# One weight chunk's scaling on VectorE, split spread rows, a 128-row mask product and a new order in an adaptive-norm block

## The chip, the cores and the metric

The kernel runs on one core of one Trainium2 chip. The metric is the device time of one execution in microseconds (us); the median of several runs is compared. The core has five engines that matter here: TensorE (PE in the profile, its weight loads PEld), VectorE (DVE), ScalarE (ACT), GpSimd (POOL), and SyncE (SP), which only issues transfers. Each works through its own list of instructions in order and waits on semaphores for the others.

## The reference

The kernel computes one transformer block with modulation from a condition vector, in float32 (cut to what matters here):

```python
mod = (_silu(L0_c) @ L0_wmod).reshape(L0_c.shape[0], 6, 1, -1)
sa, ca, ga, sb, cb, gb = (mod[:, 0], mod[:, 1], mod[:, 2], mod[:, 3], mod[:, 4], mod[:, 5])
ga = (2 * (ga >= 0) - 1) * jnp.maximum(jnp.abs(ga), 0.25)     # gb likewise
h = _layernorm(x, axis=-1) * (1 + ca) + sa
x = x + ga * _L0_attn_ref(h, ...)
h = _layernorm(x, axis=-1) * (1 + cb) + sb
x = x + gb * _L0_ffn_ref(h, L0_ffn_weight, L0_ffn_bias)
```

`x` has 8 batches of 1024 rows of 512. `_L0_ffn_ref` quantizes rows and weight in blocks of 32 to a small grid (6-bit values times a scale for each block) and multiplies. In `_L0_attn_ref` the reshape from heads back to rows puts what is not zero into the first 16 rows of each batch: the attention's result there comes from three rounds on 16 of 32 columns of each head, and all the other rows get only the bias `bo`.

## The kernel before, in words

So there are two branches. The long one takes the 1008 other rows of each batch: 16 groups, two for each batch, of 4 tiles of 128 or 124 rows. A group `g` goes through four steps. `load` brings x and adds the gate row `g2B` (gate times `bo`); in mode "P" the addition is an instruction for each tile, in mode "A" ScalarE copies the gate row into the tile and the transfer accumulates x onto it. `NV[g]` says how many of a group's four additions are on VectorE (with the row sum as a by-product, so that ScalarE needs no pass for the mean); the others are on GpSimd. `front` makes the norm (two ScalarE passes for each tile, small GpSimd steps for the inverse root, two VectorE steps with the rows psA and psB), the largest value of each block, and the two quantizing products on GpSimd (`q<-x,I`, `x<-q,M`); then TensorE transposes the tile into a psT bank, ScalarE rounds it to `xh`, VectorE makes the rest `xl`. `back` multiplies with the weight: for each of 4 output chunks 12 matmuls (xh with wh and wl, xl with wh) into a psO bank, which ScalarE evicts to `y`; an accumulating transfer adds x, and a store ends the group.

The short branch, `attention`, takes the 128 first rows (16 of each batch) as one tile `xs`: norm with rows spread over the partitions, projections, three rounds of attention whose logits begin with a mask product `par` x `far` and whose 16 x 4 blocks are matmuls of 32 x 32, the output product, and then the same norm, quantizing and product as the others. It uses the two psX banks.

Ahead of both stands the preparation. The weight comes in 4 chunks: largest values, scales (`prep_scale`), then in `prep_w` a scaling product, a rounding step on VectorE, a product back, transposes and the split into `wh` and `wl`. The two products of chunk `o` are on VectorE if `o` is in `WVEC`, else on GpSimd. The modulation is products of the condition with sections of `wmod` (`mod_sums`). Their rows are spread over partitions by a product with a row of the selection matrix `sel`. The rows RA and RS of the long branch and of the short branch's second norm come from `split`: two parts in float32r, by a ScalarE and a VectorE step. The rows RSA and RA1 of the short branch's first norm come from `whole`: one ScalarE step, in float32. `row_s` makes the product that spreads a row for the short branch.

All transfers of the preparation are on SP's queue, in the order of a string (`ORDER`); the mask `pm` alone is on GpSimd's, since it changes the type.

The order is a planner's. `Program.record` collects all instructions with a cost for each; `issue` gives each a due time, worked back from the due times in `DUE` (by strand: "B3.1" is chunk 1 of group 3's product, "L4" the load of group 4, "it0" a round of attention) with the weights `LAM`, and then lists them engine by engine: of the instructions that would be ready, the most urgent one, or a short wait (`WP`, `WV`, `WS`, `WE`, `WG`) for one that is more urgent. So a change of these numbers changes the order on every engine.

All recorded instructions bear one line in the profile, L205 (the call in `record`), so groups are told apart by their tiles.

Of the kernel before, what the change touches and what calls it, by code (L numbers as in the profile page):

```python
# [16 lines left out]
P = 128  # L17
D = 512
# [4 lines left out]
SA, CA, GA, SB, CB, GB = range(6)  # L23
# [1 line left out]

RATE = 405.0

LAM = {"gpsimd": 0.52, "scalar": 2.743, "sync": 1.216, "tensor": 0.595, "vector": 4.946}
MU = 529.0
LAMD = 2.333  # L30

DUE = {
    "first": -1000000.0,
    "sa": -156334.0,
    "L2": -176869.0,
    "B0.0": 26895.0,
    "B0.1": 27074.0,
    "B0.2": 26975.0,
    "B0.3": 26841.0,
    "L4": -130933.0,  # L40
    "B1.0": 38540.0,
    "B1.1": 38578.0,
    "B1.2": 32192.0,
    "B1.3": 38380.0,
    "att0": 47675.0,
    "kv0": 58850.0,
    "it0": 69907.0,
    "kv1": 81199.0,
    "it1": 92374.0,
    "kv2": 103548.0,  # L50
    "it2": 114723.0,
    "end": 109565.0,
    "end2": 120740.0,
    "B2.0": 53637.0,
    "B2.1": 47871.0,
    "B2.2": 53571.0,
    "B2.3": 53341.0,
    "B3.0": 76200.0,
    "B3.1": 65668.0,
    "B3.2": 64751.0,  # L60
    "B3.3": 65924.0,
    "B4.0": 76782.0,
    "B4.1": 80161.0,
    "B4.2": 79564.0,
    "B4.3": 78738.0,
    "B5.0": 91733.0,
    "B5.1": 92977.0,
    "B5.2": 93758.0,
    "B5.3": 91437.0,
    "B6.0": 104432.0,  # L70
    "B6.1": 127890.0,
    "B6.2": 146211.0,
    "B6.3": 105002.0,
    "F7": -6665.0,
    "B7.0": 117131.0,
    "B7.1": 117032.0,
    "B7.2": 116933.0,
    "B7.3": 116834.0,
    "L11": 45368.0,
    "B8.0": 136487.0,  # L80
    "B8.1": 136389.0,
    "B8.2": 135242.0,
    "B8.3": 136428.0,
    "B9.0": 139315.0,
    "B9.1": 139389.0,
    "B9.2": 142912.0,
    "B9.3": 139046.0,
    "B10.0": 155442.0,
    "B10.1": 157387.0,
    "B10.2": 157247.0,  # L90
    "B10.3": 155146.0,
    "L14": 106456.0,
    "F11": 79170.0,
    "B11.0": 167926.0,
    "B11.1": 167827.0,
    "B11.2": 167728.0,
    "B11.3": 167629.0,
    "L15": 89281.0,
    "F12": 101104.0,
    "B12.0": 180624.0,  # L100
    "B12.1": 195729.0,
    "B12.2": 196404.0,
    "B12.3": 178619.0,
    "B13.0": 193670.0,
    "B13.1": 194406.0,
    "B13.2": 192518.0,
    "B13.3": 184062.0,
    "B14.0": 195341.0,
    "B14.1": 205923.0,
    "B14.2": 204891.0,  # L110
    "B14.3": 205725.0,
    "B15.0": 218839.0,
    "B15.1": 216872.0,
    "B15.2": 218523.0,
    "B15.3": 218424.0,
}
START = {"tensor": 1070.0, "vector": 630.0, "gpsimd": 570.0, "scalar": 600.0, "sync": 600.0}

# [306 lines left out]
@with_exitstack  # L425
def _adaln(ctx: ExitStack, tc: tile.TileContext, t):
    ORDER = "0123AkCxSyXGsp"
    NV = [3, 2] + [0] * 14
    WARM3 = 0
    P0 = ((0,), (1,), (2, 3))  # L430
    P1 = ((0, 1), (2, 3))
# [2 lines left out]
    WARM2 = 0  # L434
    PARTS = 1
    REARLY = ()
    WVEC = ()
    WP = 1834
    WV = 0
    WS = 284  # L440
    WE = 235
    WG = 9256
    nc = tc.nc
    prog = Program(nc, tc)
    prog.wait, prog.gap = {"gpsimd": WP, "vector": WV, "scalar": WS, "tensor": WE}, WG
    V, S, G, PE, SY = (prog.engine(e) for e in ("vector", "scalar", "gpsimd", "tensor", "sync"))
# [3 lines left out]
    def new(name, shape, dt=F32):  # L450
        return sb.tile(shape, dt, name=name)
# [16 lines left out]
    psX = Ring("psX", 2, [P, D], F32, pp)  # L468
# [24 lines left out]
    first1, firstA, one16p = pka[:, 139:140], pka[:, 140:141], pka[:, 141:142]  # L493
# [50 lines left out]
    cs = new("cs", [P, 4, 32])  # L544
    G.memset(cs, 0.0)
    G.memset(eps, EPS)
    pm = new("pm", [2, P + D], F32R)
    G.dma_start(pm, t["pm"])
    G.memset(ones, 1.0)

# [101 lines left out]
    def split(name, ps, plus=False):  # L652
        r = new(name, [P, D], F32R)
        S.activation(r, ps, AF.Identity, scale=-0.5 if plus else 1.0, bias=one16 if plus else 0.0)
        V.scalar_tensor_tensor(r, ps, restA if plus else rest, r, ALU.mult, ALU.subtract)
        return r


    def whole(name, ps, plus=False):
        r = new(name, [P, D])  # L660
        if plus:
            S.activation(r, ps, AF.Identity, scale=firstA, bias=one16p)
        else:
            S.mul(r, ps, first1)
        return r


    vlr = Ring("vl", 2, [P, D])

    def flip(ps):  # L670
# [251 lines left out]
    def attention():  # L922
# [29 lines left out]
        ps = psX()  # L952
# [6 lines left out]
        for i in range(2):  # L959
            ps = psX()  # L960
# [25 lines left out]
        nm, r = ln_stats(xs)  # L986
# [3 lines left out]
        nm, r = ln_stats(h1)  # L990
# [5 lines left out]
        ps = psX()  # L996
# [82 lines left out]
        for it in range(3):  # L1079
# [213 lines left out]
```

## Time and profile before

| | |
|---|---|
| three runs | 301.08, 303.74, 301.57 us; median 301.57 |
| the profiled execution | 300.82 us, of which the span from first to last instruction is 299.0 |
| TensorE busy | 278.8 us (93% of the span), 2239 matmuls |
| weight loads | 216.1 us (72%) |
| VectorE busy | 225.3 us (75%) |
| ScalarE busy | 237.1 us (79%) |
| GpSimd busy | 239.7 us (80%) |
| granted TensorE clock | 0.963 in the mean |
| moved | 46.12 MB read, 16.78 MB written, 210 GB/s over the span |

The times of engines overlap, so none of them is a share of the span that could be saved by itself. A busy TensorE need not be at its peak, since ends of matmuls are modelled; where the rate matters, the step from one matmul's start to the next one's is the better number. Idle time of an engine costs only where something that ends the span waits for it.

### The profile page before, as it was taken

The page shows a single profiled execution, that of the slowest core. Times are in us where ns is not written, and L with a number is a line of the kernel's source. Part 1 is how long each engine was busy: PE and PEld are TensorE (multiplying, and loading weights), DVE is VectorE, ACT ScalarE, POOL GpSimd, SP SyncE. Part 2 cuts the span into 40 slices and gives each one's busy share as a digit, 9 for nine tenths or more (in the row PEclk, how much of TensorE's full clock was granted, in tenths as well). Part 3 has the DMA queues.
Part 4 walks back from the last instruction along what each step waited for, and adds up shares of the span by engine and source line. Part 5 has one row for each costly group of instructions (what it writes and reads, how often), then busy time and mean ns, then how long its engine had stood idle before and what let it go on. Part 6 is the DMA issues. An engine that isn't in the chain of part 4 may idle for free.

```text
span 299.0 us, 6185 instructions
## 1 busy us (share of the span) xinstructions
PE 278.8 (93%) x2239; PEld 216.1 (72%) x2239; DVE 225.3 (75%) x391; ACT 237.1 (79%) x541; POOL 239.7 (80%) x379
## 2 busy tenths in 40 slices
PE   7685599899999999999999999989999999999993
PEld 2333287799979777776787878766887788788782
DVE  6869686974989778977898799938796689941312
ACT  4169979998999999999899999979798699453400
POOL 2679989799599996999799999975999968897010
PEclk9786599999999999999999999999999999999998
DMA  6999995099569895738999657979599847576486
GB/s 223 341 410 390 273 305 167 0 181 260 185 158 212 294 212 187 136 139 158 275 246 255 136 191 138 260 216 208 196 176 311 203 179 136 170 212 139 170 153 263
DMA packets 14845, 63.28 MB, mean 212 GB/s; under 512 B 1630, under 2 KB 2398, under 8 KB 10848
## 3 DMA queue, kind: packets, MB, share of 16 engines
q0 software_dynamic: 3632, 25.99, 45.4%
q1 hardware_dynamic: 11184, 36.91, 32.0%
q8 instruction: 17, 0.28, 0.4%
q14 instruction: 12, 0.10, 0.1%
HBM read 46.12 MB, written 16.78 MB: 210 GB/s over the span
## 4 chain that ended last, share of the span: by engine, by line
PE 75%; POOL 8%; ACT 3%; issue 2%; DVE 1%; POOLq 0%; DVEq 0%
PE psO L205 52%; PE psX L205 13%; PE psT L205 9%; POOL x L205 4%; POOL q L205 2%; ACT L205 1%; ACT t L205 1%; POOL y L205 1%; ACT x L205 1%; ACT jk L205 0%; PE psB L205 0%; PE psA L205 0%; POOL s_u_l L205 0%; ACT y L205 0%; POOL cq L205 0%
## 5 line engine op out<-in xcount | busy, mean ns | idle before, releaser
L205 PE MATMUL psO<-xl,wh 128*128 128x512 f32 (+3 forms) x292 | 99.8, 389 | 0.0
L205 PE MATMUL psO<-xh,wh 128*128 128x512 f32 (+3 forms) x292 | 97.7, 386 | 1.5 <-ACT y L205 1.3
L205 PE MATMUL psO<-xh,wl 128*128 128x512 f32 (+3 forms) x292 | 97.8, 395 | 0.0
L205 POOL TENSOR_TENSOR x<-q,ms 128x512 f32<-128x512 fp8e4 (+1 forms) x64 | 73.6, 1258 | 0.1
L205 POOL TENSOR_TENSOR q<-x,s_I 128x512 fp8e4<-128x512 f32 (+1 forms) x64 | 72.4, 1204 | 1.0 <-DVE s_I L205 0.7
L205 ACT ACTIVATE y<-psO,cbT,gbT 128x512 f32<-128x512 f32 (+3 forms) x68 | 48.9, 722 | 23.1 <-PE psO L205 20.6
L205 PEld LDWEIGHTS psO<-xh,wh 128*128 128x128 f32 x292 | 52.7, 191 | 16.1 <-ACT y L205 3.5
L205 PE MATMUL psT<-pka,x 128*128 128x128 f32 (+1 forms) x256 | 56.0, 277 | 4.5 <-POOL x L205 4.5
L205 PEld LDWEIGHTS psO<-xh,wl 128*128 128x128 f32 x292 | 53.1, 189 | 9.4 <-issue 1.7
L205 PEld LDWEIGHTS psO<-xl,wh 128*128 128x128 f32 x292 | 52.8, 189 | 9.3 <-issue 1.2
L205 DVE TENSOR_TENSOR xl<-psT,xh 128x512 fp32r<-128x512 f32 (+1 forms) x64 | 41.1, 671 | 18.6 <-ACT xh L205 18.3
L205 DVE SCALAR_TENSOR_TENSOR x<-x,s_r_m,psB 128x512 f32<-128x512 f32 (+1 forms) x64 | 43.7, 741 | 11.2 <-POOL s_r_m L205 11.1
L205 DVE SCALAR_TENSOR_TENSOR x<-x,s_nm,psA 128x512 f32<-128x512 f32 (+1 forms) x64 | 45.2, 731 | 6.2 <-PE psA L205 3.9
L205 ACT ACTIVATE jk<-x,s_nm 128x512 bf16<-128x512 f32 (+1 forms) x64 | 46.3, 723 | 0.7
L205 PEld LDWEIGHTS psT<-pka,x 128*128 128x128 f32 (+1 forms) x256 | 35.1, 143 | 14.4 <-POOL x L205 6.9
L205 ACT ACTIVATE jk<-x 124x512 bf16<-124x512 f32 (+1 forms) x59 | 37.2, 630 | 3.5 <-POOL x L205 2.8
L205 ACT CAST xh<-psT 128x512 fp32r<-128x512 f32 (+1 forms) x64 | 34.6, 578 | 2.8 <-PE psT L205 2.3
L205 DVE TENSOR_REDUCE mr<-x 128x64 f32<-128x2048 f32 (+4 forms) x19 | 36.7, 1933 | 0.2
L205 POOL TENSOR_TENSOR x<-x,g2B 124x512 f32<-124x512 f32 (+1 forms) x19 | 25.2, 1361 | 0.2
L205 ACT COPY x<-g2B 128x512 f32<-128x512 f32 x40 | 22.6, 620 | 0.0
L205 POOL DMA_DIRECT2D y<-in_xT x15 | 13.6, 908 | 10.6 <-ACT y L205 10.5
L205 PE MATMUL psX<-ai,w 128*128 128x128 f32 x96 | 17.0, 274 | 0.0
(236 smaller groups left out, 369.2 us busy)
## 6 DMA issues: line engine op xcount, KB each, us to landing
x<-in_x POOLq DMA_DIRECT2D x10, 1024.0 KB, 10.6
y<-in_xT POOLq DMA_DIRECT2D x8, 1024.0 KB, 8.0
outT<-y SPq DMA_DIRECT2D x8, 1024.0 KB, 6.1
y<-in_xT POOLq DMA_DIRECT2D x7, 992.0 KB, 7.7
outT<-y SPq DMA_DIRECT2D x7, 992.0 KB, 7.2
x<-in_x SPq DMA_DIRECT2D x5, 1024.0 KB, 7.3
y<-in_wmod SPq DMA_DIRECT2D x16, 256.0 KB, 5.8
x<-in_wmod SPq DMA_DIRECT2D x8, 256.0 KB, 7.1
```

The lines of the kernel that those rows point to most:

```text
L205: o.fn = lambda: getattr(eng, meth)(*args, **kw)
```

## The change

It sets the two products of weight chunk 0 on VectorE, and all four gate additions of group 1 (two were there already). RSA and RA1 are made by `split` like the other rows, so that `row_s` always multiplies in float32r, and `whole` goes. The mask operands get 128 rows in place of 2, the added ones zero, and so does their transfer. The planner gets new due times, weights and waits. The diff, cut to its core (all of `DUE` has new values, some keys come and some go):

```diff
-LAM = {"gpsimd": 0.52, "scalar": 2.743, "sync": 1.216, "tensor": 0.595, "vector": 4.946}
+LAM = {"gpsimd": 0.528, "scalar": 2.496, "sync": 1.276, "tensor": 0.595, "vector": 4.937}
-LAMD = 2.333
+LAMD = 2.307
 DUE = {
...
-    "B0.0": 26895.0,
-    "B0.1": 27074.0,
+    "B0.0": 14381.0,
+    "B0.1": 13580.0,
...
-    "att0": 47675.0,
-    "kv0": 58850.0,
-    "it0": 69907.0,
+    "att0": 44379.0,
+    "kv0": 52784.0,
+    "it0": 65018.0,
...
-    NV = [3, 2] + [0] * 14
+    NV = [3, 4] + [0] * 14
...
-    WVEC = ()
-    WP = 1834
-    WV = 0
-    WS = 284
-    WE = 235
-    WG = 9256
+    WVEC = (0,)
+    WP = 1902
+    WV = 420
+    WS = 808
+    WE = 178
+    WG = 8719
...
-    pm = new("pm", [2, P + D], F32R)
+    pm = new("pm", [P, P + D], F32R)
...
-    def whole(name, ps, plus=False):
-        r = new(name, [P, D])
-        if plus:
-            S.activation(r, ps, AF.Identity, scale=firstA, bias=one16p)
-        else:
-            S.mul(r, ps, first1)
-        return r
...
-    RSA = whole("RSA", mod_sums(SA, psX()))
-    RA1 = whole("RA1", mod_sums(CA, psX()), True)
+    RSA = split("RSA", mod_sums(SA, psX()))
+    RA1 = split("RA1", mod_sums(CA, psX()), True)
...
-            PE.matmul(ps, lhsT=l.bitcast(F32) if r.dtype == F32 else l, rhs=r, start=True, stop=True)
+            PE.matmul(ps, lhsT=l, rhs=r, start=True, stop=True)
...
-    odd = np.stack([1 - odd, odd])
-    arr["pm"] = np.concatenate([odd[:, :P], -(2.0**100) * odd[::-1]], axis=1).astype(np.float32)
+    odd = np.stack([1 - odd, odd] + [0 * odd] * (P - 2))
+    arr["pm"] = np.concatenate([odd[:, :P], -(2.0**100) * odd[[1, 0] + list(range(2, P))]], axis=1).astype(np.float32)
```

More of the change, by code (lines that the diff above doesn't have):

```diff
@@ L26 @@
 RATE = 405.0
-LAM = {"gpsimd": 0.52, "scalar": 2.743, "sync": 1.216, "tensor": 0.595, "vector": 4.946}
+LAM = {"gpsimd": 0.528, "scalar": 2.496, "sync": 1.276, "tensor": 0.595, "vector": 4.937}
 MU = 529.0
-LAMD = 2.333
+LAMD = 2.307
 DUE = {
     "first": -1000000.0,
+    "w0": -177835.0,
+    "gb": -163184.0,
     "sa": -156334.0,
     "L2": -176869.0,
-    "B0.0": 26895.0,
-    "B0.1": 27074.0,
[L38 to L44, printed above, removed]
-    "att0": 47675.0,
-    "kv0": 58850.0,
-    "it0": 69907.0,
[L48 to L73, printed above, removed]
+    "B0.0": 14381.0,
+    "B0.1": 13580.0,
+    "B0.2": 16143.0,
+    "B0.3": 25635.0,
+    "L4": -137832.0,
+    "Q1": -111416.0,
+    "B1.0": 44936.0,
+    "B1.1": 44933.0,
+    "B1.2": 49148.0,
+    "B1.3": 53827.0,
+    "att0": 44379.0,
+    "kv0": 52784.0,
+    "it0": 65018.0,
+    "kv1": 76101.0,
+    "it1": 86920.0,
+    "kv2": 98124.0,
+    "it2": 110279.0,
+    "end": 104488.0,
+    "end2": 115707.0,
+    "L5": -101336.0,
+    "B2.0": 52569.0,
+    "B2.1": 47189.0,
+    "B2.2": 53125.0,
+    "B2.3": 57787.0,
+    "B3.0": 75107.0,
+    "B3.1": 70636.0,
+    "B3.2": 64915.0,
+    "B3.3": 65916.0,
+    "B4.0": 80773.0,
+    "B4.1": 81416.0,
+    "B4.2": 82211.0,
+    "B4.3": 79757.0,
+    "B5.0": 92096.0,
+    "B5.1": 88296.0,
+    "B5.2": 93710.0,
+    "B5.3": 92034.0,
+    "B6.0": 103659.0,
+    "B6.1": 127353.0,
+    "B6.2": 145615.0,
+    "B6.3": 104229.0,
@@ L74 @@
     "F7": -6665.0,
[L75 to L78, printed above, removed]
+    "B7.1": 124442.0,
+    "B7.2": 118816.0,
+    "B7.3": 115308.0,
     "L11": 45368.0,
[L80 to L92, printed above, removed]
@@ L93 @@
-    "F11": 79170.0,
[L94 to L114, printed above, removed]
@@ L115 @@
-    "B15.3": 218424.0,
+    "Q8": 32264.0,
+    "B8.1": 137319.0,
+    "B8.2": 136497.0,
+    "B8.3": 143922.0,
+    "B9.0": 121957.0,
+    "B9.1": 121795.0,
+    "B9.2": 127836.0,
+    "B9.3": 124088.0,
+    "L13": 63213.0,
+    "B10.0": 147572.0,
+    "B10.1": 156270.0,
+    "B10.2": 158092.0,
+    "B10.3": 140043.0,
+    "L14": 99823.0,
+    "F11": 79170.0,
+    "B11.0": 169421.0,
+    "B11.1": 175173.0,
+    "B11.2": 168888.0,
+    "B11.3": 171043.0,
+    "L15": 92811.0,
+    "F12": 99916.0,
@@ L116 @@
+    "B12.0": 181196.0,
+    "B12.1": 196536.0,
+    "B12.2": 197211.0,
+    "B12.3": 177629.0,
+    "Q13": 139881.0,
+    "B13.0": 193693.0,
+    "B13.1": 195475.0,
+    "B13.2": 178741.0,
+    "B13.3": 184700.0,
+    "F14": 143268.0,
+    "Q14": 164729.0,
+    "B14.0": 198000.0,
+    "B14.1": 206337.0,
+    "B14.2": 206132.0,
+    "B14.3": 206966.0,
+    "B15.0": 219327.0,
+    "B15.1": 247927.0,
+    "B15.2": 219246.0,
+    "B15.3": 219137.0,
 }
```

## The prediction

> **What bounds the kernel now.** I read the page first, then the busy times by stage, the chain of waits, and the timeline where the change acts. The head of the page:
>
> ```profile
> span 299.0 us, 6185 instructions
> PE 278.8 (93%) x2239; PEld 216.1 (72%) x2239; DVE 225.3 (75%) x391; ACT 237.1 (79%) x541; POOL 239.7 (80%) x379
> PEclk9786599999999999999999999999999999999998
> ```
>
> TensorE is busy for 93% of the span, and its clock is granted in full from the sixth of 40 slices on. Where it is not busy shows in the same times by stage (columns: window, its length, then busy us and instructions of PE, PEld, DVE, ACT, POOL; granted clock, DMA share, GB/s):
>
> ```profile
> 0.00:33.00 33.00, 21.48 (x126) 9.56 (x126) 26.03 (x70) 19.69 (x51) 22.31 (x41) 0.76 0.96 340
> 33.00:65.00 32.00, 30.08 (x213) 24.69 (x214) 25.74 (x46) 29.50 (x78) 28.99 (x72) 0.92 0.66 171
> 65.00:205.00 140.00, 138.34 (x1453) 110.13 (x1452) 116.58 (x186) 131.98 (x296) 126.72 (x185) 1.00 0.80 203
> ...
> 265.00:292.50 27.50, 27.30 (x138) 22.13 (x136) 6.26 (x11) 7.50 (x12) 10.33 (x11) 1.00 0.65 171
> ```
>
> There are two regimes. Up to 33 us TensorE has little to do: the DMA engines are 96% busy, and the other engines prepare weights, gates and group 0. From 33 us TensorE is the bound: it idles 32.00 - 30.08 = 1.9 us up to 65, then 1.7 us in 140. At the end the other engines have long finished. So TensorE time saved after 33 us is span saved, and so is an earlier start at 33 us; work moved among the others counts only if it shifts that start or makes TensorE wait.
>
> The chain of waits at the start (start, us, what), and its one bubble later:
>
> ```profile
> 28.70 1.27 POOL x L205
> 29.97 2.01 POOL q L205 x2
> 31.98 1.02 POOL x L205
> 33.04 2.12 PE psT L205 x8
> ...
> 194.21 1.50 issue
> ```
>
> The first transposes of group 0 wait for GpSimd, and ahead of its two quantizing products stands a 1.27 us addition `x<-x,g2B` of group 1. The 1.50 us late in the run is a pause in which TensorE's stream waits for nothing that the profile names.
>
> **The change, part by part.** The sum is made against the profiled execution: 300.82 us, of which 299.0 are span and 1.8 lie around it.
>
> (a) Spread rows. The rows of the short branch's first norm were made by `whole` in float32; `split` makes them float32r. A float32 row product runs as two instructions:
>
> ```profile
> 45.90 1.02 PE L205 MATMUL psX<-RA,sel 128*128 128x512 f32 x2
> 46.76 0.27 PE L205 MATMUL psT<-pka,x 128*128 128x128 f32 x1
> ```
>
> From its start to the next it takes 46.76 - 45.90 = 0.86 us. A float32r product of this width goes by every 0.23 us (start to start, psA and psB rows). Two such products: 2 x 0.63 = 1.26 us less TensorE time, in the stage where TensorE is the bound. Both ends of this price are known, so I take -1.26.
>
> What it adds is a VectorE step per row (RA from psA: 0.75 us), 1.5 us in all. For the second row it is in TensorE's way. In the new order the product of wmod that fills bank psX0 is followed by only eight transposes (0.11 each) and two half products (0.12 each), 1.1 us, before psX0 is written again; that write now waits for ScalarE (0.78), then VectorE (0.75) and three handovers of about 0.1, 1.8 us. TensorE, in order, waits 0.7 us, and behind it stand group 0's last pieces. If the transposes wait for GpSimd anyway, it is 0; if the VectorE step also stands behind the reduction ahead of it (1.2), it is 1.9. I take +0.7.
>
> (b) The mask product, three times. Timeline of TensorE around one:
>
> ```profile
> 102.53 0.38 PE L205 MATMUL psO<-xh,wh 128*128 128x496 f32 x1
> 102.85 0.49 PE L205 MATMUL psX<-pm 2*128 2x512 f32 x1
> 103.27 0.50 PE L205 MATMUL psO<-xl,wh 128*128 128x496 f32 x1
> ```
>
> The neighbours go by every 0.22 us. Here the step before it takes 0.32 (0.10 over) and its own 0.42 (0.19 over a 128-row product's 0.23). With 128 rows both should vanish: 3 x 0.28 = -0.84. The ends are -0.84 and 0, for no row shows this product with 128 rows; I take -0.84, since every 128-row product in the trace goes by in 0.23. The Trainium skill speaks against this gain: "TensorE: Matmul & The Clock Gate", section "LDWEIGHTS (loading the stationary operand)", says that a weight load's time follows the columns, not the rows of the contraction. By that rule alone two rows cost what 128 cost, and the sum would be 0.84 higher.
>
> (c) The start, up to 33.04 us. Group 1's four additions are now all on VectorE, so the 1.27 us addition at 28.70 is gone: -1.27 if the quantizing scales are there in time. They are due at about 28.5, and VectorE has two of those additions (0.7 each) less ahead of them, put behind. Against it stands the mask's load: 128 rows of 2,560 bytes, 0.33 MB in place of 5 KB, issued at 1.31 on GpSimd's queue, ahead in time of nearly all loads. The DMA engines are full from 3 us to 33 and move about 390 GB/s (410 and 390 in the page's third and fourth slices), so what lands afterwards lands 0.84 us later, and TensorE and ScalarE wait for those loads (wmod's first section lands at 10.36, and TensorE waits 1.7 us for it in all). I take -1.27 + 0.84 = -0.43. The ends: -1.27 with the load hidden; +1.1 with the addition's place filled by something else, the load in full, and 0.26 us from the scaling. That scaling, two products of chunk 0 (about 0.7 each on VectorE, 1.05 on GpSimd), is otherwise costed at nothing: GpSimd was idle after it from 10.34 to 12.25, and VectorE, 26.03 busy of 33, gets 1.4 us more. If that cover is gone, chunk 1's scale is late by up to 1.4 us and GpSimd's next product with it.
>
> The product of the first wmod section that stood between transposes and group 0's products (35.09 to 36.96) moves some products later. Before, ScalarE's copy (to 35.79) hid some 0.9 us of its 1.9; in its new place it costs 1.0, as its twin at 40.39. So nothing either way; half a microsecond if the clock comes up later.
>
> For the moved operations the trace has a warning:
>
> ```profile
> 9.29 1.05 POOL L205 TENSOR_TENSOR w<-q,ws 128x512 f32<-128x512 fp8e4 x1 [0.81 <-DVE q L205]
> 9.34 1.06 DVE L205 SCALAR_TENSOR_TENSOR wr<-ws,wM 128x48 f32<-128x48 f32 x1
> 10.43 0.21 DVE L205 SCALAR_TENSOR_TENSOR wr<-ws,wr 128x48 f32<-128x48 f32 x1
> ```
>
> Two steps of one shape: 1.06 us beside a GpSimd product, 0.21 alone. So a VectorE step that reads two tiles can stand still beside GpSimd. The Trainium skill has the rule, "SBUF — State Buffer", section "Who interferes with whom": such a VectorE step and a GpSimd step that reads SBUF exclude each other for the whole instruction. By it each of the four moved steps could hold GpSimd up for its 0.7 us, and the sum would be up to 2.8 higher.
>
> (d) The order anew. TensorE's instructions are as many as before, the tail's order is nearly the same, and on SP's queue a load of x and the short output each move ahead of one store. On GpSimd's queue the accumulating load into x4 moves between chunk 2's and chunk 3's products; it waits for four ScalarE copies, and behind it stand chunk 3's product and group 0's quantizing. ScalarE loses two accumulating passes (0.63 + 0.19) for two steps of 0.19: 1.3 us. The idle times of TensorE that a new order can touch are 0.30, 0.99 and 0.22 at 56.8, 59.5 and 61.8, together 1.5: there evictions stood on ScalarE behind copies into x1, which now stand earlier, but the norm's last step now directly follows an eviction, with 1.1 us of TensorE work against 1.6 of ScalarE's: a new wait of about 0.5. And evictions that end the smaller waits may stay: I take -0.7, ends -1.5 and +1.0. The pause at 194.21 has no cause in what is changed: 0, ends -1.5 and +1.5.
>
> The sum: -1.26 + 0.7 - 0.84 - 0.43 - 0.7 = -2.53, so 298.3 for the profiled execution. The median of the three runs is 301.57, 0.75 above that execution; so the forecast is 301.57 - 2.53, about 299.0 us.
>
> **The rivals.** First, faster by over 1%: VectorE's second spreading is covered (0), the start gains its whole 1.27, and the three waits go: -1.26 - 0.84 - 1.27 - 1.5 = -4.9, 296.7 us. For it: GpSimd, which ended the chain at the start, loses four large steps, and ScalarE 1.3 us. Against it: VectorE gains six large steps (two scalings, two additions, two spreadings) before 50 us, where it is 26.03 busy of 33 and 25.74 of 32 us.
>
> Second, slower: the accumulating load on GpSimd's queue. Its four copies (0.62 each, 2.5) now stand together on ScalarE behind chunk 1's copy; uncovered, they hold chunk 3's product and group 0's quantizing. Price: 2.5 + 0.84 for the mask's load + 0.99 for its issue = 4.3 at the start, against -1.26 - 0.84 of TensorE: +2.2, 303.8 us. It decides from a start 2.1 us later, that is, first transposes after 35.1. For it: in this stage ScalarE is busy 10 of 10 us from 20 on. Against it: the copies need only the gate row, there at 22.95.
>
> Third, the 128-row mask product does no better than the two-row one: 0.84 less gain, 299.9 us. It ends on the forecast's side.
>
> **How the numbers follow.** A measurement of this kernel can tell about 1%, 3.0 us, from no change. Forecast with the third rival, a change within 1%: 0.46. The first rival: 0.39. The second, and a slower result in general: 0.15, nearly all of it over 1%. All good ends together give -6.9, all bad ones +4.7. Two in ten left outside, the range is 295.8 to 303.0: below it lies the first rival with the pause gone too, above it the second in full. For the forecast alone it is 298.0 to 300.5.
>
> **What would show it.** Right: row products of 0.23 where 0.86 stood; three mask products with 128 rows, each at 0.23; TensorE's last product about 2.5 us before 294.2; first transposes at 32 to 33 us. Wrong: transposes after 35 us; mask products still at 0.42; TensorE idle over 1 us ahead of the second use of psX0 in 45 to 50 us, or anew in the short branch's 32x32 products, which now stand some 4 us of TensorE work earlier.

## The result, and the profile after

The changed kernel took 303.94 us (median of 20 runs, 302.92 to 305.66), the kernel before 302.19 us in the same series (20 runs, 298.49 to 305.08). The ratio is 1.0082, 95% interval 1.0062 to 1.0101: slower by 0.8% (by the two medians 1.75 us, 0.6%). The ratio leaves out runs more than 1.5% above the fastest of their kernel, and since before's runs spread widely this takes out from 0 of 26 to 14 of 29 of them, depending on the series: ratios of different series are therefore not held against each other below, but the medians are. The forecast was 299.0 us with a range of 295.8 to 303.0, so the sign was wrong and the time lies outside the range. The profiled execution of the changed kernel took 302.92 us, 301.1 of them span.

The head of its page, and its row of instruction loads (queue: packets, MB, share of 16 DMA engines):

```profile
span 301.1 us, 6178 instructions
PE 277.1 (92%) x2237; PEld 216.6 (72%) x2237; DVE 231.0 (77%) x399; ACT 235.7 (78%) x539; POOL 235.1 (78%) x375
PEclk9688579999999999999999999999999999999999
...
q8 instruction: 17, 0.28, 0.4%
```

The work moved as the diff says: GpSimd has 4.6 us less, VectorE 5.7 us more, and TensorE is busy 1.7 us less. Yet the span is 2.1 us longer, so TensorE waits more. Busy times by stage say where (columns as in the prediction: window, its length, busy us and instructions of PE, PEld, DVE, ACT, POOL; granted clock, DMA share, GB/s). First three stages of before:

```profile
33.00:45.00 12.00, 11.96 (x79) 8.71 (x80) 8.98 (x18) 9.79 (x26) 11.08 (x32) 0.80 1.06 280
45.00:60.00 15.00, 13.35 (x97) 11.53 (x96) 12.76 (x24) 14.71 (x40) 12.91 (x36) 1.00 0.23 79
...
187.00:200.00 13.00, 11.50 (x177) 8.86 (x176) 8.36 (x15) 12.01 (x27) 11.44 (x18) 1.00 0.90 253
```

The same of the changed kernel, with the long stage between:

```profile
33.00:45.00 12.00, 10.56 (x62) 8.31 (x60) 10.99 (x25) 9.00 (x26) 10.53 (x28) 0.67 1.04 289
45.00:60.00 15.00, 13.09 (x98) 11.05 (x98) 12.51 (x26) 14.57 (x39) 10.96 (x34) 1.00 0.46 120
60.00:187.00 127.00, 126.82 (x1306) 103.50 (x1306) 107.46 (x174) 120.37 (x277) 118.09 (x175) 1.00 0.74 188
187.00:200.00 13.00, 10.22 (x166) 7.21 (x165) 11.97 (x19) 10.90 (x25) 5.08 (x11) 1.00 0.74 151
```

Two stages got worse. From 33 to 45 us TensorE does 62 matmuls where it did 79, at a clock of 0.67 where it was 0.80. From 187 to 200 us it idles 2.78 us where it idled 1.50. In the 127 us between it idles 0.18 us in all. A smaller loss follows: from 200 to 292 us it idles 0.84 us where it idled 0.04.

At the start the transposes come 1.9 us earlier than before (31.11, was 33.04), better than forecast, and then the lead goes (timeline of the changed kernel: start, us, engine, line, instruction; in brackets the idle time before it and what ended it):

```profile
29.66 2.95 DVE L212 SCALAR_TENSOR_TENSOR x<-x,g2B 124x512 f32<-124x512 f32 x1
29.73 2.32 POOL L212 TENSOR_TENSOR x<-q,ms 128x512 f32<-128x512 fp8e4 x2
31.11 2.11 PE L212 MATMUL psT<-pka,x 128*128 128x128 f32 x8 [1.88 <-POOL x L212]
...
34.67 1.44 PE L212 MATMUL psO<-xh,wh 128*128 128x256 f32 x5 [1.44 <-ACT xh L212]
```

A gate addition on VectorE takes 2.95 us: it ends 0.56 after both of GpSimd's products have ended. ScalarE's next norm step needs its sum, and the `xh` roundings that TensorE needs stand behind that step on ScalarE. So the first product starts at 34.67, and TensorE runs it at half clock until 40.9 us; before, the clock was up from 37.8. Lined up by the matmuls that are left, the two kernels are within some 0.4 us of each other at 66 us and within 0.2 at 187 (their orders differ, so this is no finer than that), and at the end the changed one is 2.1 us behind. So by 187 us nothing is left of the early start and of TensorE's smaller work, and the loss comes after that.

What is lost at the end is the pause of the prediction's first part, which has grown (TensorE's timeline of before; "issue" means that TensorE waited for nothing that the profile shows):

```profile
193.02 1.19 PE L205 MATMUL psX<-t,vl 32*32 32x32 f32 x116
195.71 0.31 PE L205 MATMUL psX<-t,vl 32*32 32x32 f32 x12 [1.50 <-issue]
```

The same of the changed kernel:

```profile
193.10 0.27 PE L212 MATMUL psT<-pka,x 124*128 124x124 f32 x1
195.72 0.40 PE L212 MATMUL psO<-xl,wh 128*128 128x512 f32 x1 [2.35 <-issue]
```

The pause is 2.35 us where it was 1.50, and it stands between other instructions. It is joined by smaller waits that before did not have: 0.43 at 189.82 (VectorE's transpose of the attention weights), 0.43 at 207.63 (ScalarE's eviction) and 0.29 at 237.36 (GpSimd's quantizing).

### The profile page after: what moved, and what is told of

The parts are those of the page before. It is cut to its first block, busy times and chain, and to the rows that moved or that the text cites. A ratio compares the mean times of both kernels' runs of the same rounds, so it can differ in the third digit from the quotient of the medians.

```text
span 301.1 us, 6178 instructions
## 1 busy us (share of the span) xinstructions
PE 277.1 (92%) x2237; PEld 216.6 (72%) x2237; DVE 231.0 (77%) x399; ACT 235.7 (78%) x539; POOL 235.1 (78%) x375
## 4 chain that ended last, share of the span: by engine, by line
PE 47%; POOL 23%; DVE 16%; ACT 6%; issue 5%; DMA 1%; SPq 0%; POOLq 0%; ACTq 0%; DVEq 0%
PE psO L212 34%; POOL x L212 10%; DVE x L212 7%; PE psX L212 7%; PE psT L212 6%; POOL q L212 5%; ACT jk L212 2%; DVE mr L212 2%; POOL y L212 2%; POOL s_u_m L212 2%; DVE xl L212 1%; DMA w<-in_w 1%; POOL t L212 1%; DVE t L212 1%; PE psA L212 1%
## 5 line engine op out<-in xcount | busy, mean ns | idle before, releaser
L212 PE MATMUL psO<-xh,wh 128*128 128x512 f32 (+3 forms) x292 | 104.2, 395 | 2.0 <-ACT xh L212 1.4
L212 POOL TENSOR_TENSOR q<-x,s_I 128x512 fp8e4<-128x512 f32 (+1 forms) x64 | 74.0, 1227 | 3.9 <-DVE s_I L212 3.8
L212 PEld LDWEIGHTS psO<-xh,wh 128*128 128x128 f32 x292 | 54.3, 193 | 16.9 <-issue 3.3
L212 PEld LDWEIGHTS psO<-xl,wh 128*128 128x128 f32 x292 | 54.0, 191 | 9.6 <-issue 1.2
L212 PEld LDWEIGHTS psO<-xh,wl 128*128 128x128 f32 x292 | 53.8, 193 | 9.2 <-issue 0.8
L212 PE MATMUL psT<-pka,x 128*128 128x128 f32 (+1 forms) x256 | 58.2, 277 | 2.4 <-POOL x L212 2.2
L212 ACT ACTIVATE jk<-x 128x512 bf16<-128x512 f32 (+1 forms) x57 | 36.1, 633 | 0.5
L212 POOL TENSOR_TENSOR x<-x,g2B 128x512 f32<-128x512 f32 (+1 forms) x17 | 22.1, 1384 | 0.1
```

Source lines behind the costliest of these rows:

```text
L212: o.fn = lambda: getattr(eng, meth)(*args, **kw)
```

## The experiments

In all of them the order of instructions is written out as a list of operation numbers and held, so that an edit moves only what it names: `order = FIXED` in `issue` in place of the planner's choice. "Before's order" is the list that the planner makes for the kernel before, "after's order" that of the changed kernel. Times are medians; ratios are against the kernel before on the same chip, where its medians were 302.19 to 302.59 us. There were five series: e1 to e4, e5 to e8, e9 to e12, e13 to e15, and e16 with e17. A trace is one execution, and executions of one kernel differ by 1 to 7 us. Kernels with the same start (e8, e12, e15 and e17) have their first transposes between 30.97 and 31.63 us, so half a microsecond between two traces shows little.

### Which part costs

The TensorE part alone, in before's order:

```diff
+        order = FIXED                       # before's order
-    pm = new("pm", [2, P + D], F32R)
+    pm = new("pm", [P, P + D], F32R)
-    RSA = whole("RSA", mod_sums(SA, psX()))
-    RA1 = whole("RA1", mod_sums(CA, psX()), True)
+    RSA = split("RSA", mod_sums(SA, psX()))
+    RA1 = split("RA1", mod_sums(CA, psX()), True)
```

> The kernel before with only the split spread rows and the 128-row mask product; the instruction order of before is written out and held, with VectorE's two new spreading steps put right behind their ScalarE steps. Theory A (TensorE is the bound, so its saved work is saved time, and the loss of the change comes from its order and its start): after's trace shows 0.23 in place of 0.86 for two row products (-1.26) and 0.23 to 0.32 in place of 0.42 for three mask products (-0.45), so 1.2 to 1.7 us faster than before, less where the 0.33 MB mask load delays the start. Theory B (the saved work is lost again in waits wherever it is saved, as for the second spread row): within 0.4 us of before.

Measured: 302.74 us, 1.0037 [1.0001, 1.0074]. The forecast's gain did not come, although its pieces did: lined up with before, the row products save 0.52 and 0.53 us and the three mask products 0.92 together. But the first transposes come at 33.57 instead of 33.04, TensorE waits 0.62 us at 45.88 for a VectorE copy behind the new spreading steps, and its pause late in the run is longer, too (1.89 us).

All four parts of the code in before's order:

```diff
 (e1_te_only, and)
-    NV = [3, 2] + [0] * 14
+    NV = [3, 4] + [0] * 14
-    WVEC = ()
+    WVEC = (0,)
```

> All four code parts of the change (scaling of chunk 0 and group 1's additions on VectorE, split rows, 128-row mask), in the order of before, written out and held. Theory A (the new order costs, late in the run): about 1 us faster than before, and 2 to 3 us faster than after; the pause near 195 us is 1.5 to 1.7 as in before. Theory C (the additions on VectorE beside GpSimd's products cost the start, whatever the order): no faster than before, and the first transposes of group 0 no earlier than 33.0.

Measured: 302.24 us, 1.0026 [0.9994, 1.0059]. When the third round's second product begins, this kernel is 1.1 us ahead of before (191.89 us, where it was 193.02); then it pauses 1.94 us, and the clock drops (window 196 to 200):

```profile
196.00:200.00 4.00, 4.00 (x12) 2.49 (x11) 0.46 (x3) 4.00 (x10) 2.96 (x7) 0.57 0.49 102
```

Twelve matmuls in 4 us at 0.57 of the clock, after which it is 0.84 us behind. In this execution a late pause eats the gain.

The order alone, with before's code:

```diff
+        order = FIXED                       # after's order
```

> The code of before (additions and scaling on GpSimd, float32 rows, two-row mask) in the order of after, written out and held; where an operation changes its engine it keeps its place. Theory A: the order alone costs 2 to 3.5 us against before, with the longer pause (2.4 us or more) near 195 us and the late start of group 0. Theory C: within 0.7 us of before.

Measured: 304.74 us, 1.0115 [1.0054, 1.0175]. Its transposes come at 29.31. One VectorE gate addition, one that was on VectorE before the change too, takes 2.66 us at 28.15, so the lock beside GpSimd comes from where the order puts the addition. Then TensorE waits 2.25 us ahead of 42.39 for ScalarE's eviction. The longer pause near 195 us that was expected is not in this trace (next section).

### The pause

The trace's packets of the instruction queue point to its cause. The queue moves blocks of 16,384 bytes. In before, after, e1, e2 and e6 TensorE stops behind the same recorded instruction, its 3521st (weight loads, matmuls and semaphore waits counted together), whatever instruction that is, and goes on 2.2 to 2.5 us after such a packet starts: 193.20 then 195.71 in before, 193.53 then 195.72 in after, 194.22 then 196.53 in e1, 192.69 then 195.04 in e2, 193.25 then 195.46 in e6. In before, 17 packets for 4,541 recorded instructions make 267 each, or 252 if a first block was there without a packet (an estimate). The third round's second product is about as much: 64 products of 32 x 32 in two passes each, 128 matmuls with their weight loads, are 256 recorded instructions in some 1.3 us.

e3 shows that the count alone is not enough. It has after's order and the same burst, and no pause at that count:

```profile
192.20 1.29 PE L273 MATMUL psX<-t,vl 32*32 32x32 f32 x128 [0.31 <-DVE t L273]
...
194.45 0.85 PE L273 MATMUL psO<-xh,wl 128*128 128x512 f32 x3
195.25 0.32 PE L273 MATMUL psT<-pka,x 124*128 124x124 f32 x1
```

There the packet starts at 192.40, 0.2 us after the burst's start, and TensorE reaches its 3521st instruction at 194.94, 2.5 us later. In after the packet starts 3.7 us after the burst's start, when the 3521 instructions are used up. So the pause is what is left, when TensorE reaches that count, of the 2.2 to 2.5 us from the packet's start. To test it, idle products ahead of the burst shift it against the block's edge:

```diff
+            if it == 2:
+                av = psX()
+                with prog.together():
+                    for i in range(10):
+                        for h in range(4):
+                            PE.matmul(av[r, o], lhsT=qw[r, o], rhs=ksT[it][r, o], start=True, stop=True, ...)
 ...
-            av = psX()
+            av = av if it == 2 else psX()
```

> After, its order held, plus 40 idle 32x32 products (80 TensorE instructions, about 0.35 us) right behind the third round's logits, into the bank that the round's second product overwrites. In both traces the late pause begins behind TensorE's 3521st recorded instruction and ends 2.2 to 2.5 us after a 16 KB instruction load began. Code-loading theory: the pause comes where the 256 instructions of one block of code are 32x32 products that run in 1.1 us, faster than the next block is loaded; 80 more instructions ahead split the third round's product over two blocks, the pause of 2.35 us goes, and the kernel is 1.7 to 2.1 us faster than after. Rival (the pause is a wait on data or a clock event at that time): it stays, and the kernel is 0.3 us slower than after.

Measured: 300.93 us, 0.9989 [0.9957, 1.002], 3.0 us less than the changed kernel for more work. (A float32 product is two passes with a weight load each, so the idle products are 160 recorded instructions and take about 0.8 us, not 80 and 0.35.) No pause is left:

```profile
190.00 1.29 PE L280 MATMUL psX<-t,vl 32*32 32x32 f32 x128 [0.33 <-DVE t L280]
193.30 0.27 PE L280 MATMUL psT<-pka,x 124*128 124x124 f32 x1
193.33 0.48 PE L280 MATMUL psO<-xl,wh 128*128 128x512 f32 x1
```

The same idle products in the kernel before:

```diff
+        order = FIXED                       # before's order
+            if it == 2: (the idle products)
```

> Before, its order held, plus the 40 idle 32x32 products (80 TensorE instructions) behind the third round's logits. Code-loading theory: before has the same pause, 1.50 us, and loses it too: 1.1 to 1.5 us faster than before, and the spread of its runs (298.2 to 304.8) shrinks, since the time at which the block of code lands is what varies. Then the longer pause explains about 1 us of what after lost, and after with the idle products (300.9) is still 0 to 1 us slower than this. Rival (the pause is only that long in the order of after): no change.

Measured: 300.74 us, 0.9954 [0.9927, 0.9981]. So before loses to the pause too, but less: 1.45 us (302.19 to 300.74) against 3.01 in the changed kernel (303.94 to 300.93). The difference, 1.56 us, is most of the 1.75 us that the change costs by the medians. By the ratios, of two series, it is 0.47 of 0.82 points. Nor is this kernel free of pauses: in its profile a pause has appeared elsewhere, behind a block load at 163.19:

```profile
164.25 0.39 PE L273 MATMUL psO<-xl,wh 128*128 128x512 f32 x1
165.53 0.39 PE L273 MATMUL psO<-xl,wh 128*128 128x512 f32 x1 [0.89 <-issue]
```

### Order or code

With the idle products in each, the order can be told from the code. All code parts in before's order:

```diff
 (e2_code_old_order, and)
+            if it == 2: (the idle products)
```

> All four code parts in the order of before, held, as in the second run, plus the 40 idle products (a float32 product is two passes with two weight loads, so 160 recorded instructions, some 0.7 us). With the late pause gone from both, this against after with the idle products (300.9) is the price of the new order alone. Order theory: after had lost 0.9 us to this kernel's start by 66 us and had waits of 0.67 and 0.4 at 207 and 237 us that the old order has not, so this is 0.7 to 1.5 us faster: 299.4 to 300.2. Rival (the pause was all that the order cost): the same as 300.9 within 0.4.

Measured: 301.81 us, 0.998 [0.9957, 1.0003], no faster than e4's 300.93: with all its code the new order costs nothing beyond the pause. And it is no faster than e5's 300.74: in before's order the four code parts bring nothing, although the late pause is gone (a pause of 0.51 us stands at 181.29 instead). Before's code in after's order:

```diff
+        order = FIXED                       # after's order
+            if it == 2: (the idle products)
```

> The code of before in the order of after, held, plus the 40 idle products: the fourth corner of a square with the late pause out of the way. The corners so far, against before: old code and old order 0.995, new code and old order 0.998, new code and new order 0.999. Theory D (new code and new order each cost little by themselves once the pause is gone; what the code saves on TensorE it pays in waits): this is 0.995 to 1.000. Rival (the new order needs the new code: with the additions of group 1 on GpSimd it loses at 42 us what its early start brings, as the run without the idle products showed with a wait of 2.2 us): 1.004 to 1.010.

Measured: 306.50 us, 1.0174 [1.0126, 1.0223]. The new order without the new code is bad: TensorE idles 1.96 us ahead of 43.85 for ScalarE's eviction, and its clock is 0.64 from 33 to 45 us. The order and the code belong together.

### The lead at the start

The long VectorE addition taken out of the changed kernel's start:

```diff
 (after's order, with two of group 1's VectorE additions and the four ScalarE steps
  that read their sums moved behind the second `xh` rounding)
```

> After, its order held, except that VectorE's first two additions of group 1 and ScalarE's four steps that use them stand behind group 0's copies xh, so behind GpSimd's two products instead of beside them. Port theory (the addition at 29.66 took 2.95 us because VectorE and GpSimd exclude each other, and ScalarE's copies xh stood in order behind it): the addition takes 0.7, the first product of group 0 starts about 1 us earlier than 34.67, and 0.5 to 1.3 us is left of it at the end. Rival (the products wait for ScalarE's other copies anyway, and group 1 comes later): within 0.4 us of after.

The addition is short now, and the first product starts 0.25 us earlier although the transposes came 0.52 later:

```profile
34.01 0.68 DVE L280 SCALAR_TENSOR_TENSOR x<-x,g2B 124x512 f32<-124x512 f32 x1
...
34.42 1.43 PE L280 MATMUL psO<-xh,wh 128*128 128x256 f32 x5 [0.68 <-ACT xh L280]
```

But the time is 304.12 us, 1.0055 [1.0032, 1.0077]: a longer pause (2.42 us, to 195.46) and a clock of 0.66 in 196 to 200 cover what it brought. With the pause out of the way:

```diff
 (e4_shift with e6_adds_after's move)
```

> After with the idle products, and with VectorE's first two additions of group 1 behind group 0's copies: the earlier experiment on the additions, with the late pause out of the way. Port theory: the 2.95 us addition cost the start 0.6 to 0.8 us (the earlier run gained 0.78 at the first product, 0.6 by 42 us), and that stays to the end: 300.1 to 300.5 against 300.9. Rival (TensorE meets the same waits later, group 1 among them): 300.9 within 0.3.

Measured: 301.16 us, 0.9954 [0.9931, 0.9978], the same as e4 (300.93). In its profile the first product is 0.80 us earlier than e4's, and by 41.49 the lead is gone in a wait for an eviction. More of the start repaired:

```diff
 (e10_shift_adds, with the product of wmod back between group 0's transposes and
  products, and the mask's load moved from the start to about 82 us)
```

> The same, and in addition the product of wmod for the spread row RSA stands between the transposes and the first products again, as in before, and the mask's load is issued at about 82 us. Theory (in the order of after this product cost its whole 1.9 us at half clock inside the stream, and the mask's load 0.5 us of the start): 1.5 to 2 us faster than without these two, about 298.5. Rival (what stands ahead of the products is hidden behind the copies xh in both): at most 0.5 us faster, by the mask's load.

Measured: 300.11 us, 0.9923 [0.9889, 0.9956]. At 39.6 us it is 2.05 us ahead of e10; then TensorE waits 1.2 us for VectorE's spreading of RSA and 0.7 us for an eviction, and at the end it is 0.13 us ahead. That is one execution of each; by the medians of the same series e11 is 1.05 us faster, so something of the earlier start may be kept. Those two waits taken away:

```diff
 (e11_repaired, with group 0's first two evictions ahead of group 1's norm steps on
  ScalarE, and the spreading of RSA earlier)
```

> The kernel of the eleventh run (order of after, idle products, additions behind xh, wmod product early, mask late), and in addition ScalarE's first two evictions of group 0 ahead of group 1's third and fourth mean and square steps, and RSA's two spreading steps ahead of what delayed them. In the eleventh run TensorE, with its earlier start, waited 1.2 us for VectorE's spreading of RSA (at 39.90) and 0.7 us for the eviction (at 41.42), which stood behind group 1's steps. Theory E (the earlier start of after is lost there: VectorE's additions for group 1 pace ScalarE, and ScalarE's order makes the evictions wait): both waits go, TensorE is 1.2 to 1.9 us earlier at 42 us, and 0.5 to 1.5 us remain at the end, 298.6 to 299.6. Rival (another wait of the same size follows at once, for group 1's own steps): 300.1 within 0.4.

Measured: 301.78 us, 0.9996 [0.996, 1.0033]. Both waits went, TensorE was 2.78 us ahead at 38.64, ran out of work and stood still:

```profile
45.44 0.48 PE L280 MATMUL psT<-pka,x 128*128 128x128 f32 x1 [2.94 <-POOL x L280]
```

It waits for the second half of group 0 on GpSimd, and in e11 the same transposes start at 45.24. And the long idle time is followed by a lower clock: 0.68 in 45 to 60 us, where e11 had 1.00. (The profiled execution, 303.75 us, is the slowest of the twelve.) So in this order there is a floor at about 45 us that TensorE's lead alone does not pass.

### The version that beats both

The TensorE parts with their covers, in before's order:

```diff
 (e1_te_only, with the idle products, the mask's load at about 78 us, and the VectorE
  copy `bdc` ahead of the spreading steps)
```

> The kernel with only the split rows and the 128-row mask, in the order of before, as in the earlier run that was no faster, but with the three waits that it showed taken away: the mask's load is issued on GpSimd's queue at about 78 us, in a gap of 3.5 us, instead of at 1.3 us; VectorE's copy bdc, which held TensorE up for 0.8 us behind the spreading steps, moves ahead of two steps; and the 40 idle products shift the code blocks. Theory A (the saved TensorE work of 1.7 us is there and was eaten by these waits: 0.55 at the start, 0.8, 0.4 more in the pause): 2.5 to 3.5 us faster than before. Theory B (saved work in the short branch is lost in any case): no better than before with the idle products alone.

Measured: 300.69 us, 0.9967 [0.994, 0.9995], no better than e5 without the TensorE parts. Transposes at 33.03, where e1 had 33.57; two new pauses at block loads (0.70 us to 107.36, 0.63 us to 181.59). With the VectorE parts added:

```diff
 (e7_te_covered, and)
-    NV = [3, 2] + [0] * 14
+    NV = [3, 4] + [0] * 14
-    WVEC = ()
+    WVEC = (0,)
```

> The same, with the scaling of chunk 0 and group 1's additions on VectorE too: all four code parts of the change, in the order of before. In the order of before these two parts moved the first transposes from 33.57 to 32.55. If that lasts, this is about 1 us faster than the kernel without them, 3.5 to 4.5 us faster than before, about 298; if TensorE then waits for VectorE elsewhere, it is the same as without them.

Measured: 299.89 us, 0.9915 [0.9888, 0.9943]; transposes at 31.38. Against e7, in the same series, that is 0.80 us for the VectorE parts; against e9 (301.81), which differs from it by the mask's load and the copy only, 1.9 us. A pause of 0.64 us remained, now inside the third round's logits. So the burst itself was cut:

```diff
 (e8_all_covered without the idle products, and)
+            parts = 4 if it == 2 else PARTS
-            for i0 in range(0, 16, 16 // PARTS):
+            for i0 in range(0, 16, 16 // parts):
 (eight other TensorE operations between the parts, the output product later by as many)
```

> The fastest kernel so far (all code parts in the order of before, mask loaded late, bdc early, 299.9), but without idle products: the third round's second product is cut into four parts with eight other TensorE products between two of them, and the output product behind it stands seven products later. Code-loading theory: cutting the burst is enough, since one block of code then lasts some 6 us; the 0.7 us of idle products and a pause of 0.83 us among them go: 0.8 to 1.5 us faster, about 298.8. Rival: the later output product makes the short branch late and TensorE waits for it at the end: the same or slower.

Measured: 299.05 us, 0.9896 [0.9857, 0.9936], the fastest of all, without idle products. Its burst runs in four parts without a pause; two of them:

```profile
190.30 0.45 PE L273 MATMUL psX<-t,vl 32*32 32x32 f32 x32
...
192.94 0.45 PE L273 MATMUL psX<-t,vl 32*32 32x32 f32 x32
```

In its trace TensorE is 2.2 us ahead of before at 42 us, 1.9 at 60 and 2.4 at the end, so here an earlier start is kept. GpSimd is earlier with it: its quantizing of group 0's second half ends at 44.1 us, where before's ends at 46.0. The cut of the burst was not tried by itself.

One eviction that TensorE still waited for was moved in it:

```diff
 (e12_all_split, with the eviction of group 0's last chunk ahead of three copies on ScalarE)
```

> The fastest kernel so far (299.05), with one step of ScalarE moved: the eviction of group 0's last chunk stands ahead of three copies and a mean step instead of behind them. TensorE waited 1.1 us for it at 57.60, as at 59.47 in before, which is the wait that I expected the new order to remove. If the removal of such a wait is worth its length, 0.8 to 1.2 us faster, about 298.0; if the copies, now 0.45 later, hold a load that TensorE waits for, the same.

Measured: 300.12 us, 0.9961 [0.9924, 0.9997], no gain. In e12 the wait was 0.99 us ahead of 57.60:

```profile
57.60 0.72 PE L273 MATMUL psO<-xh,wh 128*128 128x248 f32 x4 [0.99 <-ACT y L273]
```

Here that product starts at 56.55, and 2.6 us later another wait has taken its place:

```profile
59.16 0.66 PE L273 MATMUL psX<-pka,h 128*128 128x128 f32 x4 [1.08 <-ACT h L273]
```

That is the short branch's own chain, which is no earlier. Last, each TensorE part of the change was undone in e12. The spread rows:

```diff
-    RSA = split("RSA", mod_sums(SA, psX()))
-    RA1 = split("RA1", mod_sums(CA, psX()), True)
+    RSA = whole("RSA", mod_sums(SA, psX()))
+    RA1 = whole("RA1", mod_sums(CA, psX()), True)
```

> The fastest kernel (299.05, ratio 0.990) with the split rows alone undone: RSA and RA1 by one ScalarE step in float32 again, order held. TensorE then does 1.06 us more between 44 and 50 us, and VectorE two steps of 0.75 less. Floor theory (up to 60 us the end of a stretch is set by group 0's second half on GpSimd and by the short branch's chain, not by TensorE): within 0.5 us of the fastest kernel. TensorE theory, that of the prediction: 1.0 to 1.3 us slower.

Measured: 299.18 us, 0.9929 [0.9895, 0.9962]: the same as e12 (299.05), though in another series with intervals of about 1 us. The traces agree: level within 0.1 us at 50 us and at the end. So the split rows are worth nothing that shows here. The mask:

```diff
-    pm = new("pm", [P, P + D], F32R)
+    pm = new("pm", [2, P + D], F32R)
```

> The fastest kernel with the 128-row mask product alone undone: two rows, and its load of 5 KB, order held, the load at 78 us as there. In the run of the TensorE parts alone the three products and the steps before them took 0.24, 0.39 and 0.29 us less with 128 rows. Both theories: TensorE is the bound at 103, 140 and 178 us, so 0.7 to 1.0 us slower than the fastest kernel. If it is the same, the saved time there is lost later too, in the pauses for code.

Measured: 300.26 us, 0.9945 [0.992, 0.9971], some 1.2 us slower than e12 and 1.1 slower than e16, which ran in the same series. Its trace falls behind e12's by 0.40, 0.40 and 0.19 us at 101, 137 and 176 us, where the mask products are, 1.0 us in all. (Another 0.6 us is there before 36 us and 0.4 comes at 162; these are not the mask's.) The intervals overlap at their edges; the trace's steps decide.

## Why the prediction was wrong

**The bound.** "So TensorE time saved after 33 us is span saved, and so is an earlier start at 33 us" is the first step that failed, for the stage from 33 to 60 us. It was read from 1.9 us of idle time in 32, as if a nearly busy engine had to be the bound. Up to about 60 us TensorE only runs level with three others: GpSimd's second half of group 0 (near 45 us, shown by e14), ScalarE's evictions, which stand behind group 1's steps (41 to 44 us: e10, e11, e13), and the short branch's chain (59 us: e15). Whoever moves TensorE alone ahead there turns busy time into a wait. The floors are not fixed: in e12, where GpSimd's second half came 1.9 us earlier too, 1.9 of a lead of 2.2 us passed 60 us. After 60 us the sentence holds: the mask's saving is kept (e17), unless a pause eats it: e7 has the mask product too and is level with e5 (300.69 and 300.74).

**(a) Spread rows**: rightly sized, worth nothing. The row product of RA1 in the changed kernel and, ahead of it, the wait for the second row's spreading:

```profile
47.75 0.49 PE L212 MATMUL psX<-bdc,pkb 128*128 128x128 f32 x2 [0.40 <-DVE RA L212]
...
49.07 0.39 PE L212 MATMUL psX<-RA,sel 128*128 128x512 f32 x1
49.30 0.38 PE L212 MATMUL psX<-ck__162,pkb 128*128 128x128 f32 x2
```

The step is 49.30 - 49.07 = 0.23 us, as predicted. TensorE waits 0.40 us for VectorE's spreading, 0.56 over the normal step; predicted was 0.7. But of the -1.26 + 0.7 nothing reaches the end (e16), since all of it lies before 60 us.

**(b) The mask product**: right. In the changed kernel:

```profile
99.90 0.48 PE L212 MATMUL psO<-xh,wl 128*128 128x512 f32 x1
100.22 0.39 PE L212 MATMUL psX<-pm 128*128 128x512 f32 x1
100.45 0.39 PE L212 MATMUL psO<-xh,wl 128*128 128x512 f32 x1
```

Its own step is 0.23 us where it was 0.42 (0.32 in the third place); the step ahead of it keeps its 0.32 in two of the three places. That gives about 0.6 of the 0.84 us in these rows; the same rows of e1 give 0.74, lined up with before 0.92, and e17's median 1.2. The Trainium skill's rule on weight loads ("TensorE: Matmul & The Clock Gate", section "LDWEIGHTS (loading the stationary operand)"), which would have made this 0, agrees with the weight load itself: 181 ns with 2 rows, 186 to 192 with 128. The product is what is slow with two rows, and of that the rule says nothing.

**(c) The start**: the transposes came at 31.11, 1.93 us earlier, where 0.43 was forecast. The mask's load can cost the start: with it late (and `bdc` moved) the first transposes come 1.09 us earlier in e8 than in e9 (31.38, 32.47); the 0.54 us from e1 to e7 (33.57, 33.03) are within what two traces differ by. In the changed kernel it was not moved by itself, so what it costs there is not shown. The lead was then lost behind the addition of 2.95 us. The prediction had shown that a VectorE step can stand still beside GpSimd and named the rule ("SBUF — State Buffer", section "Who interferes with whom"), but it charged GpSimd with it. Here VectorE was the one held, by two GpSimd products in a row, and the price was in what stood behind it: the norm step and the roundings on ScalarE. "Half a microsecond if the clock comes up later" was too little: it came up at 40.9, not 37.8.

**(d) The order anew**: -0.7 was wrong as a saving. Waits of this stage can be removed, but they come back at the next floor (e15). The order as such is not what made the kernel slow (e4 is no slower than e9), except through the pause.

**The pause** "has no cause in what is changed: 0 (±1.5)" is the step that decides the sign. Its cause is the edge of a code block, and the bounds were too narrow: in the changed kernel 0.85 us more idle time in one profile, and by e4 and e5 1.56 of the 1.75 us between the medians. The Trainium skill describes such blocks ("Runtime: NRT & Kernel Launch", section "🔬 Instruction fetch mechanics"): 16 KiB, 256 instructions, fetched ahead by the engine's own queue, the crossing "mostly hidden". The packets of this trace agree with the block's size; the crossing isn't hidden here, 1.50 and 2.35 us. Why the block's load starts late in the changed kernel was not tried. Its burst begins at 189.82 and the load at 193.53, while accumulating loads keep the DMA engines full in both kernels; that the load stands behind them is a supposition, and e3 speaks against it: there they are as full (DMA share 0.86 to 1.15 in each microsecond from 189 to 195), and the load starts at once. Open too is the rest of the loss: e4 (300.93) and e5 (300.74) are 0.2 us apart by the medians and 0.35 points by the ratios, whose intervals overlap, and e5 has a pause of 0.89 us elsewhere that e4 has not; the half clock at the start and the waits at 207 and 237 us are candidates.

**The rivals.** None of the three happened: the start was early, not late; the mask product did gain; and the gain of the first rival did not come through. The slower case was laid on GpSimd's queue, and it came from TensorE's own instruction supply; that its 303.8 us is close to the measured 303.94 is luck.

## What to carry to other kernels

Before TensorE time is counted as span, look at each stage for the next two engines that would stop it: an engine that is nearly always busy beside others that are 85 to 98% busy (as here from 45 to 60 us before the change) is not yet the bound, and a saving there is worth what the nearest floor lets through. An idle time that the profile puts down to "issue" deserves a look at the instruction queue's packets: if it stands behind a fixed number of instructions in version after version, it is probably a block's edge, and moving instructions ahead of it tests that. A burst of very short instructions ahead of it is worth cutting up: the fastest kernel here (0.9896 [0.9857, 0.9936]) has that, together with the mask's load moved off the start. When versions are compared, the pause should be taken out of all of them first; otherwise a change is judged by where it happens to put the edge.

## What the hardware showed that was not expected

A burst of 256 short TensorE instructions in 1.3 us outran the instruction supply, and the stop came at the same instruction count in five kernels with different lists of instructions; in e3, which reached that count 2.5 us after the packet's start, there was none. A pause of some 2 us can be followed by a drop of the granted clock (0.57 in e2, 0.66 in e6, in the 4 us from 196 on), though not always: before, after and e1 kept 1.00 (pauses of 1.50, 2.35 and 1.89 us). An idle time of 2.94 us ahead of 45.44 (e14) went with a clock of 0.68 in the mean from 45 to 60 us. And a VectorE step of 0.68 us can last 2.95 us when two GpSimd products run one behind the other beside it.
